# First attention of a hybrid block: units taken in pairs, in a written order, with the next batch's normalization in parts

## The chip, the cores and the metric

The kernel runs on one core of a Trainium2 chip. The metric is the device time of one execution in microseconds (us). Three executions gave 4361.11, 4361.49 and 4366.51 us, so the median is 4361.49. One more execution was taken by the hardware profiler; it is the one that all views of the profile show.

The core has several engines that run side by side, each through its own list of instructions: TensorE (PE in the profile; its weight loads are listed apart as PEld) multiplies matrices into PSUM, VectorE (DVE), ScalarE (ACT) and GpSimd (POOL) work on rows of data, and SyncE (SP) issues the transfers from and to memory. An instruction waits until what it reads has been written and until the buffer that it writes is free.

## The reference

The input x has 8 batches of 512 tokens of 256 features, all in float32. Four residual sublayers follow one another. The change is in the first:

```python
x = x + attn_a(_layernorm(x), Wq, Wkv_down, Wk_up, Wv_up, Wo)   # 8 heads of 64, one latent of 64
x = x + ffn(_layernorm(x), ...)      # two layers of local attention and a gated feedforward
x = x + attn_b(_layernorm(x), ...)   # 16 heads of 16
x = x + ffn(_layernorm(x), ...)

def attn_a(x, Wq, Wkv_down, Wk_up, Wv_up, Wo):
    q = (x @ Wq.T).reshape(b, t, 8, 64)
    kv_latent = x @ Wkv_down.T                       # b, t, 64
    k = (kv_latent @ Wk_up.T).reshape(b, t, 8, 64)
    v = (kv_latent @ Wv_up.T).reshape(b, t, 8, 64)
    attn = softmax(einsum('bqhd,bkhd->bhqk', q, k) * 64 ** -0.5)
    out = einsum('bhqk,bkhd->bqhd', attn, v).reshape(b, t, 512)
    return out @ Wo.T
```

## The kernel before

**Stages.** The eight batches go in two groups of four. For each group the stages run one behind the other: first attention, two layers of local attention and feedforward, second attention, the two layers again. Every stage is a generator of steps, and the last steps of a stage call `ahead()`, which runs single steps of the opening (`head()`) of the next one. What a stage's Python code emits first is first in an engine's list unless the scheduler, which places instructions by their dependences and the order in which they were emitted, finds something that can go earlier. `order_keeper` (line 245) overrides that: inside `with kept_order():` every instruction is tied to the one before it on its engine, in the order of the text. First attention doesn't use it in the kernel before.

**First attention** (`attention_a`, lines 311 to 485). The keys' and the queries' matrices are folded into one, and so are the values' and the output's, so a head's scores are a product of 64 folded query columns with the latent, and its values are the latent weighted by the probabilities. For each batch a `prologue` prepares three tiles: `latT` (latent, features on the partitions), `lat` (tokens on the partitions) and `qT` (folded queries). It yields after each part: the layer norm (statistics line 279, the inverse root on POOL line 267, scaling line 287), two transpositions with their copies (lines 299 and 353), the latent (358, 360), its transposition (364, 366) and four products for `qT` (374, 377). All of them share one PSUM buffer, `ps_mm`, with the projection.

**A unit** is two heads of 128 query rows against all 512 keys. A batch has 4 x 4 = 16 units, a group has 64. A unit has five parts:

- `scores`: two matmuls (line 393) into a tile `s`; the negated maximum of both heads by one DVE reduction (397); two exponentials on ACT (241, through the helper `function`), which also give the sums;
- `divide`: a DVE reciprocal of the two sums (409) and two multiplications on ACT (411);
- `turn`: eight 128x128 transposes on PE (418) into a tile `ppt`, and one DVE copy to `pt` (420);
- `values`: eight pairs of matmuls (429) into a quarter of the PSUM tile `o`; every fourth unit copies the full `o` to `oT` on ACT (439);
- `project`: every fourth unit multiplies `oT` with the folded output matrix (447) into `pp`, and adds that to x on DVE (448).

**The order** is one unit to a step. In step n the code emits `divide` of unit n-1, `scores` of unit n, `turn` of unit n-2, one piece of the next batch's prologue, `values` of unit n-3 and `project` of unit n-4:

```python
if step % each == 2 and step // each + 1 < len(batches):
    pieces = prologue(batches[step // each + 1])
for part in (1, 0, 2, 3, 4):
    at = step - part
    if 0 <= at < len(units):
        got[at] = units[at][part](*got.get(at, ()))
    if part == 2:
        next(pieces, None)
```

**Buffers.** PSUM: `s` and `ppt` share three buffers (`ps_s`), `o` has one, `mm` (prologue and projection) has one. In SBUF: `p` (probabilities) has three buffers, `pt` three, `two` (latT, oT and others) seven, `sums` three.

**Rotation tables** (`rotation_tables`, line 217) are for the local attention of the next stages. They are made once, between the opening and the steps of the first stage: two transfers, into `raw` (a buffer of the tag `p`) and `sc` (of the tag `two`), and eight DVE multiplications (227) in one run.

Of the kernel before, what the change touches and what calls it, by code (L numbers as in the profile page):

```python
# [17 lines left out]
P = 128  # L18
# [20 lines left out]
GELU_TABLES = "gelu_and_others"  # L39
Piece = namedtuple("Piece", "heavy first act second dve late", defaults=(None, None, None, None, None))  # L40
Unit = namedtuple("Unit", "n product inverse error refine masks squares masked highest exponentials turn keep_turned values project")
ISSUE_ORDER = mybir.DependencyInfo(mybir.DependencyClass.NoSync, mybir.DependencyReason.DATA)
WAIT = mybir.DependencyInfo(mybir.DependencyClass.Sync, mybir.DependencyReason.SCHED_ONLY)

# [2 lines left out]
def kernel(  # L47
# [168 lines left out]

    def rotation_tables():

        raw = pool.tile([P, 4, NT, HD], F32, tag="p", name="raw", bufs=3)
        nc.sync.dma_start(raw, rope.rearrange("c (t p) d -> p c t d", p=P))  # L220
        sc = pool.tile([P, DEPTH, 4, HD], F32, tag="two", name="sc", bufs=7)
        nc.sync.dma_start(
            sc.rearrange("p l c d -> p (l c d)"), f_scale.rearrange("l c d -> (l c d)").partition_broadcast(P)
        )
        for l in range(DEPTH):
            for c in range(4):
                nc.vector.tensor_mul(tabs[l][:, c], raw[:, c], sc[:, l, c].unsqueeze(1).to_broadcast([P, NT, HD]))

    tabs = [const.tile([P, 4, NT, HD], F32, name=f"tab{l}") for l in range(DEPTH)]

    phase = {"start": None, "last": [], "gates": False, "opening": False}
# [59 lines left out]
    def layernorm(halves, dst, name):  # L291

        normalize_rows(halves, dst, *row_statistics(halves, name)[1:])
# [17 lines left out]
    def attention_a(batches, g):  # L311
# [3 lines left out]
        def fold():  # L315
# [16 lines left out]
            for half in range(2):  # L332
# [8 lines left out]
                for odd in range(2):  # L341
                    rows = slice(odd * HD, (odd + 1) * HD)
                    nc.vector.tensor_copy(wvo_a[rows, 2 * half : 2 * half + 2, :], pw[rows, odd])

        def prologue(b):

            n = f"a{b}"
            yr = pool.tile([P, NT, D], F32, tag="yr", name=f"yr_{n}", bufs=1)
            layernorm([xs[b]], [yr], n)
            yield  # L350
            yT = pool.tile([P, 2, T], F32, tag="hT", name=f"yT_{n}")
            for k in range(2):
                nc.scalar.copy(yT[:, k, :], transposed(ps_mm, halves_of(yr), k, f"pyt_{n}_{k}"))
                yield

            pd = ps_mm.tile([P, T], F32, tag="mm", name=f"pd_{n}")
            for k in range(2):
                nc.tensor.matmul(pd, lhsT=wd_a[:, k, :], rhs=yT[:, k, :], start=(k == 0), stop=(k == 1))
            latT = pool.tile([P, T], F32, tag="two", name=f"latT_{n}", bufs=7)
            nc.vector.tensor_copy(latT, pd)  # L360
            yield
            pl = ps_mm.tile([P, NT, HD], F32, tag="mm", name=f"pl_{n}")
            for t in range(NT):
                nc.tensor.transpose(pl[:, t, :], latT[:HD, t * P : (t + 1) * P], ident[:HD, :HD])
            lat = pool.tile([P, NT, HD], F32, tag="lat", name=f"lat_{n}")
            nc.scalar.copy(lat, pl)
            yield
            qT = big([P, 4, T], f"qT_{n}")
            if b == batches[0]:
                fold()  # L370
            for m in range(4):
                pq = ps_mm.tile([P, T], F32, tag="mm", name=f"pq_{n}_{m}")
                for k in range(2):
                    nc.tensor.matmul(
                        pq, lhsT=wqk_a[:, k, m * P : (m + 1) * P], rhs=yT[:, k, :], start=(k == 0), stop=(k == 1)
                    )
                nc.scalar.copy(qT[:, m, :], pq)
                state[b] = qT, latT, lat
                yield

        def unit(b, i, u):

            n = f"a{b}_{i}_{u}"

            def scores():
                qT, latT, lat = state[b]
                if u == 0:
                    state["sums"] = pool.tile([P, H], F32, tag="sums", name=f"sums_{n}", bufs=3)
                sums = state["sums"]
                s = ps_s.tile([P, 2, T], F32, tag="s", name=f"s_{n}")  # L390
                for odd in range(2):
                    rows = slice(odd * HD, (odd + 1) * HD)
                    nc.tensor.matmul(  # L393
                        s[:, odd], lhsT=qT[rows, u, i * P : (i + 1) * P], rhs=latT[rows, :], start=True, stop=True
                    )
                nm = pool.tile([P, 2], F32, tag="nm", name=f"nm_{n}", bufs=4)
                nc.vector.tensor_reduce(nm, s, AX.X, ALU.max, negate=True)  # L397
                p = pool.tile([P, 2, T], F32, tag="p", name=f"p_{n}", bufs=3)
                for odd in range(2):
                    h = 2 * u + odd  # L400
                    function(
                        p[:, odd], s[:, odd], AF.Exp, bias=nm[:, odd : odd + 1], accum_out=sums[:, h : h + 1]
                    )
                return p, sums, lat

            def divide(p, sums, lat):

                some = sums[:, 2 * u : 2 * u + 2]
                nc.vector.reciprocal(some, some)  # L409
                for odd in range(2):  # L410
                    nc.scalar.activation(p[:, odd], p[:, odd], AF.Identity, scale=some[:, odd : odd + 1])  # L411
                return p, lat

            def turn(p, lat):
                ppt = ps_s.tile([P, 2, NT, P], F32, tag="s", name=f"ppt_{n}")
                for odd in range(2):
                    for k in range(NT):
                        nc.tensor.transpose(ppt[:, odd, k, :], p[:, odd, k * P : (k + 1) * P], ident)  # L418
                pt = pool.tile([P, 2, NT, P], F32, tag="pt", name=f"pt_{n}", bufs=3)
                nc.vector.tensor_copy(pt, ppt)  # L420
                return pt, lat

            def values(pt, lat):
                if u == 0:
                    state["o"] = ps_o.tile([P, 4, P], F32, tag="o", name=f"o_{n}")
                o = state["o"]
                for k in range(NT):
                    for odd in range(2):
                        nc.tensor.matmul(  # L429
                            o[odd * HD : (odd + 1) * HD, u, :],  # L430
                            lhsT=lat[:, k, :],
                            rhs=pt[:, odd, k, :],
                            start=(k == 0),
                            stop=(k == NT - 1),
                        )
                if u < 3:
                    return ()
                oT = pool.tile([P, 4, P], F32, tag="two", name=f"oT_{n}", bufs=7)
                nc.scalar.copy(oT, o)
                return (oT,)  # L440

            def project(oT=None):
                if oT is None:
                    return
                pp = ps_mm.tile([P, D], F32, tag="mm", name=f"pp_{n}")
                for k in range(4):
                    nc.tensor.matmul(pp, lhsT=oT[:, k, :], rhs=wvo_a[:, k, :], start=(k == 0), stop=(k == 3))
                nc.vector.tensor_add(xs[b][:, i, :], pp, xs[b][:, i, :])

            return scores, divide, turn, values, project  # L450

        units = [unit(b, i, u) for b in batches for i in range(NT) for u in range(4)]
        each = NT * 4
        def steps(ahead):
            tables_of(EXP_TABLES)
            got, pieces = {}, iter(())
            for step in range(len(units) + 4):
                if step % each == 2 and step // each + 1 < len(batches):
                    pieces = prologue(batches[step // each + 1])
                for part in (1, 0, 2, 3, 4):  # L460
                    at = step - part
                    if 0 <= at < len(units):
                        got[at] = units[at][part](*got.get(at, ()))
                    if part == 2:
                        next(pieces, None)
                if step > len(units) - 6:
                    ahead[0]()
                yield

# [1 line left out]
        rest = steps(follower)  # L471

        def head():
            yield from prologue(batches[0])
            while phase["gates"]:
                yield
            for _ in range(EARLY_STEPS):
                next(rest)
                yield

        def run(ahead):
            follower.append(ahead)
# [1234 lines left out]
```

## Time and profile before

| what | value | where it is from |
| --- | --- | --- |
| median of three runs | 4361.49 us | the times |
| the profiled execution | 4372.94 us | the times |
| its span | 4371.1 us | the profile's first line |
| PE busy in the whole span | 4122.6 us, 94% | busy time of the engines |
| first attention, first group (27 to 308 us): PE, DVE, ACT busy | 277.9, 190.6, 201.7 us of 281 | busy time by stretches |
| first attention, second group (2195 to 2480 us): PE, DVE, ACT busy | 282.7, 192.1, 202.0 us of 285 | the same |
| the exponentials, line 241, p from s and nm | 256 of 682 ns | costliest groups |
| the divisions, line 411 | 256 of 720 ns | costliest groups |
| the maxima, line 397 | 128 of 1223 ns | costliest groups |
| the copies of the transposes, line 420 (60 to 290 us) | 55 of 1214 ns | groups of a window |
| the copies of o, line 439 (60 to 290 us) | 14 of 582 ns | groups of a window |

The span is the time from the first to the last instruction of the profiled execution, and the execution's own time has 1.8 us around it. The two stages of first attention are 566 of 4371 us. A table of stretches gives, for a stretch of time, how long each engine was busy in it and how many instructions it ran; a group puts all instructions of one line and shape together; the chain lists what the end of a stretch waited for, followed back. In all of them `PE s_a L393 x4` means four matmul instructions of line 393 into the tile s_a.

### The profile page before, as it was taken

Reading aid. Unit: us, or ns where it says so; the run is one execution under the profiler, and the core shown is the slowest. Engines: PE = TensorE matmul, PEld = TensorE weight load, DVE = VectorE, ACT = ScalarE, POOL = GpSimd, SP = SyncE. Lnnn points to the kernel's source line nnn. Section 1 sums busy time; section 2 is a strip of 40 time slices with the busy share of each in tenths; the row PEclk is TensorE's granted clock in tenths of the full one; section 3 lists DMA queues with packets and bytes.
Section 4 is the critical chain, followed back from the end, with each engine's and each line's share of the span. In section 5 each row is a group of like instructions: output and inputs, shape, how many; then the busy total and the mean of one; then the engine's idle time right before and its main releaser. Section 6 shows DMA issues by size and latency. Waiting matters only on the chain.

```text
span 4371.1 us, 70487 instructions
## 1 busy us (share of the span) xinstructions
PE 4122.6 (94%) x26580; PEld 2578.8 (59%) x26580; DVE 3069.1 (70%) x7505; ACT 2686.5 (61%) x6316; POOL 1144.6 (26%) x1140
## 2 busy tenths in 40 slices
PE   8999999999998899999999999999999988999999
PEld 5666656655555466566566666566555554665665
DVE  6678737746999887377466786477379997864773
ACT  6777517616989675276167775276179896752761
POOL 0014314312222343143200242143122223422431
PEclk9999999999999999999999999999999999999999
DMA  2000000000000000000100000000000000000000
GB/s 83 1 23 4 23 3 23 3 25 21 2 1 1 20 4 7 3 23 14 53 30 1 20 4 24 23 3 24 5 21 1 1 1 20 4 6 23 3 4 24
DMA packets 51091, 63.36 MB, mean 14 GB/s; under 512 B 6336, under 2 KB 45504, under 8 KB 50752
## 3 DMA queue, kind: packets, MB, share of 16 engines
q1 hardware_dynamic: 50752, 58.85, 4.1%
q8 instruction: 211, 3.46, 0.3%
q14 instruction: 128, 1.05, 0.1%
HBM read 46.28 MB, written 4.19 MB: 12 GB/s over the span
## 4 chain that ended last, share of the span: by engine, by line
PE 67%; DVE 21%; ACT 10%; issue 1%; POOL 1%; DMA 0%; SPq 0%; POOLq 0%; ACTq 0%; DVEq 0%
PE pu_g1x L1042 3%; PE pu_g0y L1042 3%; PE pu_g1y L1042 3%; PE pu_g0x L1042 3%; PE s_a L393 3%; PE o_a L429 3%; PE ppt_a L418 3%; ACT r_b L241 2%; PE pqk_f1x L514 2%; PE pqk_f0x L514 2%; PE pqk_f1y L514 2%; PE pqk_f0y L514 2%; DVE pt_b L1389 2%; PE ppt_b L1384 2%; ACT num_b L241 2%; DVE r_b L1335 2%
## 5 line engine op out<-in xcount | busy, mean ns | idle before, releaser
L1384 PE MATMUL ppt_b<-ident,num_b 128*128 128x128 f32 x1280 | 223.5, 291 | 88.0 <-DVE pt_b L1389 65.3
L1384 PEld LDWEIGHTS ppt_b<-ident,num_b 128*128 128x128 f32 x1280 | 137.6, 143 | 273.4 <-ACT num_b L241 98.7
L241 ACT ACTIVATE num_b<-num_b,most_b 128x512 f32<-128x512 f32 (+3 forms) x512 | 280.7, 552 | 22.0 <-POOL most_b L1364 21.7
L1389 DVE COPY pt_b<-ppt_b 128x512 f32<-128x512 f32 (+1 forms) x352 | 224.3, 637 | 28.5 <-PE ppt_b L1384 27.8
L241 ACT ACTIVATE p_a<-s_a,nm_a 128x512 f32<-128x512 f32 x256 | 173.5, 682 | 105.1 <-DVE nm_a L397 101.9
L1331 DVE TENSOR_TENSOR t_b<-den_b,r_b 128x1024 f32<-128x1024 f32 (+1 forms) x176 | 197.5, 1122 | 45.4 <-ACT r_b L241 44.9
L1354 DVE CUSTOM_DVE_ANT_0 num_b<-num_b,r_b 128x512 f32<-128x512 f32 (+3 forms) x512 | 226.2, 490 | 1.9 <-POOL num_b L1347 1.9
L1347 POOL TENSOR_TENSOR num_b<-num_b,causal 128x256 f32<-128x256 f32 (+2 forms) x176 | 174.0, 988 | 186.3 <-ACT num_b L1341 185.7
L1312 PE MATMUL den_b<-st_b,st_b 18*128 18x384 f32 (+3 forms) x1024 | 208.5, 472 | 0.4 <-ACT num_b L1341 0.4
L397 DVE TENSOR_REDUCE nm_a<-s_a 128x2 f32<-128x1024 f32 x128 | 156.4, 1223 | 70.6 <-PE s_a L393 70.6
L1335 DVE SCALAR_TENSOR_TENSOR r_b<-t_b,r_b 128x1024 f32<-128x1024 f32 (+1 forms) x176 | 204.9, 1164 | 0.2
L1312 PE MATMUL dot_b<-st_b,st_b 16*128 16x384 f32 (+3 forms) x1024 | 189.6, 472 | 6.2 <-ACT yT_b L1190 4.4
L411 ACT ACTIVATE p_a<-p_a,sums_a 128x512 f32<-128x512 f32 x256 | 171.9, 720 | 26.5 <-DVE sums_a L409 26.5
L241 ACT ACTIVATE r_b<-den_b 128x1024 f32<-128x1024 f32 (+1 forms) x176 | 165.7, 941 | 35.1 <-PE den_b L1312 17.5
L241 ACT ACTIVATE p_f0y<-p_f0y,nm_f0y,rn_f0y 128x256 f32<-128x256 f32 (+1 forms) x256 | 143.7, 563 | 63.2 <-DVE nm_f0y L653 63.2
L1341 ACT ACTIVATE num_b<-dot_b 128x1024 f32<-128x1024 f32 (+1 forms) x176 | 164.6, 935 | 28.3 <-PE dot_b L1312 28.3
L241 ACT ACTIVATE p_f1y<-p_f1y,nm_f1y,rn_f1y 128x256 f32<-128x256 f32 (+1 forms) x256 | 143.7, 564 | 61.3 <-DVE nm_f1y L653 61.3
L1364 POOL TENSOR_SCALAR most_b<-most_b 128x2 f32<-128x2 f32 (+2 forms) x176 | 34.0, 193 | 557.1 <-DVE most_b L1354 541.8
L241 ACT ACTIVATE p_f0x<-p_f0x,nm_f0x,rn_f0x 128x256 f32<-128x256 f32 (+1 forms) x256 | 143.7, 563 | 57.7 <-DVE nm_f0x L653 57.7
L241 ACT ACTIVATE p_f1x<-p_f1x,nm_f1x,rn_f1x 128x256 f32<-128x256 f32 (+1 forms) x256 | 143.7, 564 | 56.3 <-DVE nm_f1x L653 56.3
L241 ACT ACTIVATE r_b<-r_b 128x1024 f32<-128x1024 f32 (+1 forms) x176 | 172.4, 980 | 5.6
L556 POOL TENSOR_TENSOR ro_f1x<-ro_f1x,rs_f1x 128x512 f32<-128x512 f32 x64 | 80.2, 1274 | 355.5 <-DVE sums_f1x L726 182.0
(356 smaller groups left out, 11230.4 us busy)
## 6 DMA issues: line engine op xcount, KB each, us to landing
x<-in_x SPq DMA_DIRECT2D x8, 512.0 KB
out<-x SPq DMA_DIRECT2D x8, 512.0 KB
wf_0x<-in_f_wqkv SPq DMA_DIRECT2D x2, 1536.0 KB
wf_0y<-in_f_wqkv SPq DMA_DIRECT2D x2, 1536.0 KB
wf_1x<-in_f_wqkv SPq DMA_DIRECT2D x2, 1536.0 KB
wf_1y<-in_f_wqkv SPq DMA_DIRECT2D x2, 1536.0 KB
wg_0x<-in_f_w SPq DMA_DIRECT2D x2, 1386.0 KB
wg_0y<-in_f_w SPq DMA_DIRECT2D x2, 1386.0 KB
```

The lines of the kernel that those rows point to most:

```text
L241: i = nc.scalar.activation(out, in_, func, **more).ins
L411: nc.scalar.activation(p[:, odd], p[:, odd], AF.Identity, scale=some[:, odd : odd + 1])
L514: nc.tensor.matmul(dst.rearrange("p h d -> p (h d)"), lhsT=hTs[b][:, k, t * P : (t + 1) * P], rhs=wqkv[:, k, c * INNER : (c + 1) * INNER], ...
L1042: nc.tensor.matmul(pu[: cols.stop - cols.start, c], lhsT=w1[:, k, cols], rhs=hT[:, k, :], start=(k == 0), stop=(k == 1),)
L1312: return nc.tensor.matmul(s[:, a, m * width : (m + 1) * width], lhsT=left[at, j, past:width], rhs=right[at, j, :width], start=True, stop=True,
L1331: nc.vector.tensor_mul(t[:, :, :cols], den[:, :, :cols], r[:, :, :cols])
L1335: nc.vector.scalar_tensor_tensor(r[:, :, :cols], t[:, :, :cols], 2.0, r[:, :, :cols], ALU.subtract, ALU.mult)
L1341: nc.scalar.activation(num[:, :, :cols], dot[:, :, :cols], AF.Square, scale=-0.5)
L1347: nc.gpsimd.tensor_add(own, own, mask)
L1354: nc.vector.tensor_tensor_reduce(out=s4[:, a, m, :], in0=s4[:, a, m, :], in1=r4[:, a, m, :], scale=-1.0, scalar=LOWEST, op0=ALU.mult, op1= ...
L1384: nc.tensor.transpose(ppt[:, k, :], p[:, a, k * P : (k + 1) * P], ident)
L1389: nc.vector.tensor_copy(pt[:, a, :nblocks, :], ppt[:, :nblocks, :])
```

## The change

First attention now goes by pairs of units, 32 to a group, with eight steps to a batch, and inside a step all engines keep the order of the text. A unit's parts are cut finer (the namedtuple `UnitA`): the maxima, the inversions, the copies of transposes, the copy of o and the addition are parts of their own. In step m the pair m is new (its units are A and B below), pair m-1 is turned (C and D), pair m-2 is weighted (E and F). The text's order is: scores A, B; values E, F; maxima A, B; a part of a normalization or one table multiplication; exponentials A, B; in odd steps the copy of o; inversion A; transposes C and their copy; a piece of the prologue; divisions A; transposes D; inversion B; the copy of D's transposes; divisions B; in odd steps the projection and its addition; another piece. So a step may run two pieces of the prologue, and a prologue now starts in the fifth step of the batch before.

The prologue's layer norm has become a generator of its own (`normalized`): statistics of two tiles of tokens at a time, then scalings of two at a time, one part to a step, between the maxima and the exponentials. The eight table multiplications go into a list (`later`) that is taken from singly in the last three steps of a batch, in steps in which no normalization part is left. `raw` and `sc` take buffers of other tags. In the last steps of a stage `ahead()` is called twice for each pair step; `head()` runs one pair step where it ran two unit steps.

```diff
-        raw = pool.tile([P, 4, NT, HD], F32, tag="p", name="raw", bufs=3)
+        raw = pool.tile([P, 4, NT, HD], F32, tag="rs", name="raw", bufs=1)
...
-        sc = pool.tile([P, DEPTH, 4, HD], F32, tag="two", name="sc", bufs=7)
+        sc = pool.tile([P, DEPTH, 4, HD], F32, tag="ro", name="sc", bufs=3)
...
-        for l in range(DEPTH):
-            for c in range(4):
-                nc.vector.tensor_mul(tabs[l][:, c], raw[:, c], sc[:, l, c].unsqueeze(1).to_broadcast([P, NT, HD]))
+        def table(l, c):
+            nc.vector.tensor_mul(tabs[l][:, c], raw[:, c], sc[:, l, c].unsqueeze(1).to_broadcast([P, NT, HD]))
+        later.extend(lambda l=l, c=c: table(l, c) for l in range(DEPTH) for c in range(4))
...
+        def normalized(b):
+            some = None
+            for tokens in (range(2), range(2, NT)):
+                some = row_statistics([xs[b]], f"a{b}", tokens, some)
+                yield
+            state["yr"] = pool.tile([P, NT, D], F32, tag="yr", name=f"yr_a{b}", bufs=1)
+            for tokens in (range(2), range(2, NT)):
+                normalize_rows([xs[b]], [state["yr"]], *some[1:], tokens)
+                yield
...
         def prologue(b):
             n = f"a{b}"
-            yr = pool.tile([P, NT, D], F32, tag="yr", name=f"yr_{n}", bufs=1)
-            layernorm([xs[b]], [yr], n)
-            yield
+            yr = state["yr"]
...
+            for m in range(len(pairs) + 2):
+                new, turning, weighted = pair(m), pair(m - 1), pair(m - 2)
+                done = weighted[1] if weighted and m % 2 else None
+                following = m // each + 1
+                with kept_order():
+                    for some in new:
+                        some.scores()
+                    for some in weighted:
+                        some.values()
+                    for some in new:
+                        some.maxima()
+                    if m % each == (m < each) and following < len(batches):
+                        rows = normalized(batches[following])
+                    if next(rows, rows) is rows and later and m % each > 4:
+                        later.popleft()()
+                    for some in new:
+                        some.exponentials()
+                    if done:
+                        done.keep_values()
+                    if new:
+                        new[0].invert()
+                    if turning:
+                        turning[0].turn()
+                        turning[0].keep_turned()
+                    if m % each == 4 and following < len(batches):
+                        pieces = prologue(batches[following])
+                    next(pieces, None)
+                    if new:
+                        new[0].divide()
+                    if turning:
+                        turning[1].turn()
+                    if new:
+                        new[1].invert()
+                    if turning:
+                        turning[1].keep_turned()
+                    if new:
+                        new[1].divide()
+                    if done:
+                        done.project()
+                        done.add()
+                    next(pieces, None)
+                if m > len(pairs) - 3:
+                    ahead[0]()
+                    ahead[0]()
+                yield
...
         def head():
+            yield from normalized(batches[0])
             yield from prologue(batches[0])
             while phase["gates"]:
                 yield
-            for _ in range(EARLY_STEPS):
-                next(rest)
-                yield
+            next(rest)
+            yield
```

## The prediction

> **What bounds the kernel now.** The change touches the first attention alone, which runs twice, at about 27 to 308 us and 2195 to 2480 us. I read the busy time by stretches there first, then the chain that ended last, then the timeline, for who hands over to whom.
>
> Busy time by stretches: length; busy us of TensorE (PE), its weight loads (PEld), VectorE (DVE), ScalarE (ACT), GpSimd (POOL), each with its count of instructions; granted clock, DMA share, GB/s. Three rows from later stages are for the clock, below.
>
> ```profile
> core 0: us, PE busy (x) PEld busy (x) DVE busy (x) ACT busy (x) POOL busy (x), PEclk, DMA share, GB/s
> 150.00:180.00 30.00, 30.00 (x252) 20.10 (x252) 22.55 (x32) 25.12 (x55) 1.20 (x2) 1.00 0.00 1
> ...
> 2488.45:2491.86 3.41, 2.00 (x17) 1.23 (x14) 3.38 (x15) 0.75 (x3) 3.33 (x3) 1.00 0.00 0
> 2491.86:2495.27 3.41, 3.41 (x5) 1.35 (x5) 2.97 (x13) 3.17 (x10) 0.09 (x2) 0.50 0.00 0
> 3027.74:3031.15 3.41, 1.58 (x12) 1.22 (x10) 2.97 (x12) 3.14 (x10) 0.00 (x0) 1.00 0.01 2
> ```
>
> PE is busy all 30 us, ACT 25 and DVE 23. A busy PE may still be waiting, so the chain decides (start, length, what):
>
> ```profile
> 157.21 1.02 PE ppt_a L418 x8
> 158.24 1.02 PE o_a L429 x16
> 159.26 1.92 PE pp_a L447 x8
> 161.18 1.06 PE s_a L393 x4
> 162.24 1.02 PE ppt_a L418 x8
> 163.27 1.02 PE o_a L429 x16
> 164.29 1.06 PE s_a L393 x4
> ```
>
> Only PE stands in it: scores 1.06, transposes 1.02, values 1.02, so 3.11 us a unit (scores start at 164.22, 167.33, 170.43 in the timeline), and every fourth unit a projection of 1.92: 4 x 3.11 + 1.92 = 14.35 for four units (the timeline's scores from 213.9 to 228.2 say the same). PE binds; whatever makes it wait is paid in full.
>
> The timeline gives the hand-overs (start, length, engine, line, what; in brackets the idle time before and who ended it):
>
> ```profile
> 164.22 1.13 PE L393 MATMUL s_a<-latT_a,qT_a 64*128 64x512 f32 x4
> ...
> 165.40 1.23 DVE L397 TENSOR_REDUCE nm_a<-s_a 128x2 f32<-128x1024 f32 x1 [0.20 <-PE s_a L393]
> ...
> 166.66 0.69 ACT L241 ACTIVATE p_a<-s_a,nm_a 128x512 f32<-128x512 f32 x1
> ...
> 168.13 0.17 DVE L409 RECIPROCAL sums_a<-sums_a 128x2 f32<-128x2 f32 x1 [0.38 <-ACT p_a L241]
> 168.34 1.33 ACT L411 ACTIVATE p_a<-p_a,sums_a 128x512 f32<-128x512 f32 x2 [0.23 <-DVE sums_a L409]
> ...
> 300.73 1.23 DVE L420 COPY pt_a<-ppt_a 128x1024 f32<-128x1024 f32 x1 [0.17 <-PE ppt_a L418]
> ...
> 305.48 0.58 ACT L439 COPY oT_a<-o_a 128x512 f32<-128x512 f32 x1 [3.87 <-PE o_a L429]
> ...
> 306.12 2.00 PE L447 MATMUL pp_a<-wa,oT_a 128*128 128x256 f32 x8
> ```
>
> Scores to maximum: 1.18. Maximum to exponentials: 1.26. Two exponentials hold ACT for 1.34. Transposes (299.65 in the timeline) to their copy: 1.08. Copy of o, 0.58, and 0.06 later the projection.
>
> **What is saved.** Inside a group the trace's single matmuls start 0.109 apart (transposes, value pairs) or 0.43 (512 columns): 2 x 0.43 + 8 x 0.109 + 8 x 0.109 = 2.61 of work in the 3.11 of a unit. The other 0.50 lies at the three changes of shape (64 rows, 128x128, 64 columns): the last matmul before one holds 0.09 longer, the first behind it 0.05 to 0.10. A pair step keeps the order scores A and B, values E and F, transposes C and D (A, B new; C, D the pair before; E, F the one before that): three changes for two units, 2 x 2.61 + 0.48 = 5.70. The projection, now between transposes and scores, adds only its 8 x 0.216 = 1.73 instead of 1.92. A double step (four units) is 5.70 + 7.43 = 13.13 of PE: 1.22 under 14.35. 16 double steps in each of two stages: **-39 us**, if PE never waits. The built program's instruction order does have this order on PE.
>
> **What is added: two waits.** I lay one step out from 0, the start of A's scores. PE: A 0 to 0.96, B to 1.91, E and F to 3.80, C to 4.73, D to 5.60. DVE: maximum A at 1.18, B 1.16 later at 2.34, done at 3.57. ACT: exponentials A 2.44 to 3.78. Exponentials B could follow, but the tag p has three buffers: C and D hold two, A took the third, so B writes where C's transposes read. The waits that the built program carries name exactly this. C's last transpose starts at 4.62, lasts 0.27 (the median of the tile's rows) and hands over in 0.05 to 0.1: B's exponentials run 5.0 to 6.35.
> In odd steps the copy of o stands behind them on ACT: 6.35 to 6.93. The projection behind it on PE starts at 7.0, where PE was ready at 5.60: **1.40 of stall**. The divisions queue behind the copy (6.95 to 9.6); they are wanted by the next transposes only, 3.8 after the next start at 8.8.
> In even steps the next scores want the PSUM buffer of C's transposes (three buffers, four tiles a step): the copy starts at 3.86 + 1.08 = 4.95, lasts 1.22, hands over at 6.2, where PE was ready at 5.70: **0.50**. A plain double step thus costs 15.03, not 13.13.
>
> In steps 4 to 7 of a batch, a next batch's prologue fills part of this. Step 4: the second transposition needs the one PSUM buffer mm, whose copy stands behind B's exponentials (6.35 to 6.93): 0.9. Steps 5 and 7: the product (four matmuls, 1.72) between C and D hides most of the projection's wait, but the piece behind the projection waits for its addition (0.25 hand-over, 0.43): 0.8 and 0.9 with what remains. Step 6: 0. Together 2.65 against 3.80.
> Per stage, from step 2: one plain double step, then 2.65, 3.80, 2.65, 3.80, 2.65 and four plain: 1.9 + 15.55 + 7.6 = 25.1; two stages: **+50**.
>
> **Moved work.** Normalization by two rows of tokens (four statistics at 0.4, or two scalings at 0.35) is 0.8 of DVE between maximum B (free at 3.5) and the copy of C (4.95): hidden by 0.65. The rotation tables (2.76 for eight at 40.88) go singly into the same gap. Their tags (rs, ro for p, two) free a p buffer at the start only; SP issues as many DMAs as before. In the third batch the next stage's statistics (0.8 to 1.2 a step) use that gap up: copy of C 0.65 late once, 0.2 once: +0.9 a stage, +2. Their cover gone everywhere, 0.8 in eight steps of three batches would be at most 0.15 each beyond the gap, nothing more.
> **Opening.** The first transposes wait for four exponentials and a division. Following the first stage from its second scores (32.8) by the same durations, step 2 starts at 42.3, and PE reaches at 48.4 what it had in the before at 47.0, short of 0.88 of the prologue's transposes: 2.3 late, though 1.5 double steps should have gained 1.6: +4. In the second stage the previous feedforward's output (ten us of PE) covers the first step; two waits of 1.0 and 1.4 remain against the 1.1 there now: +1.3. Bounds 0 and +8 for both. **Drain.** Last projection 0.5, the next stage's first products waiting for their columns 0.7: +1.2 a stage, bounds -1 and +4 (the existing wait of 1.29 at 294.87 there may grow).
>
> **Sum:** -39 + 50 + 2 + 5.3 + 2.4 = **+21** against the profiled execution (span 4371.1, 4372.9 in all): 4394. That execution is 11 above the median of the runs, so the forecast goes by the median: 4361.5 + 21 = **4382**.
>
> **Two rules weighed.** The page Perfetto Trace Analysis of the Trainium skill (Identifying the Most-Contended Engine) says to judge TensorE's headroom by the share of weight loads, not by busy matmuls. The first stretch has 20.10 of 30: by it a third of PE is free, the stalls would vanish in it and the sum would be -39. The chain without a gap speaks against it; I go by the chain.
> On the clock, the trace: 2488.45 to 2491.86 is 2.00 busy of 3.41, and the next 3.41 run at 0.50; 3027.74 to 3031.15, with 1.58 busy, 8 of its 12 matmuls transposes, is followed by no drop. The page TensorE: Matmul & The Clock Gate (Part 4: PE-mode transpose) says that transposes do not count as busy in the same way. By it C, D and the stall behind them are 3.2 us of idling in each plain odd step, and its half rate would come each time. The row with eight transposes contradicts that, and I take nothing for it.
>
> **Rivals.** *PE stays fed:* were the two waits covered, the sum would be -39 and the time 4322; any wait of less than 1.22 us a double step still leaves a gain. For it: ACT and DVE have 5 and 7 us free in 30. Against it: the waits come of the order, not of the load. 7%. *The two cancel:* hand-overs overlap more than I read, the stalls are 1.2 and not 1.9 a plain double step (and 0.6 of what they are elsewhere): 50 falls to 31, the sum is +2, 4363. 15%. *The clock falls:* each odd step without a prologue, 9 a stage, loses half of a 3.41 window, 1.7: +31 on top, 4413; the shown rows put the edge between 1.58 and 2.00 modelled us of 3.41, which overlaps, so it can't be excluded; the odd step has 3.41 - 1.40 = 2.0. 5%. *The order is undone by the scheduler:* excluded by the built order.
>
> **How the numbers follow.** Forecast 73%, 4370 to 4400: hand-overs of 0.05 each way on some 50 stalls are 3, the opening and drain bounds -7 to +8. About 0.2% (8.7 us) is what this kernel's runs can tell. The range 4358 to 4403 leaves out the fed PE, some of the cancelling and most of the clock's case. Faster 0.09 (fed, 0.07, and a little of the cancelling), same 0.13 (the rest of it), slower 0.78 (forecast and clock).
>
> **What would show it.** In the chain of the after: PE broken by ACT, projections released by the copy of o some 1.4 late in plain odd steps, scores released by the copy of the transposes 0.5 late; exponentials waiting for ppt_a; scores of two units 1.9 long in one run. Wrong, if projections follow the transposes at once, if the plain double step is under 14.35, or if the clock drops in the first attention.

## The result, and the profile after

The changed kernel took 4406.1 us (median of four executions, 4394.46 to 4406.74), the kernel before 4364.0 in the same comparison (4361.11 to 4373.17). The ratio is 1.0087, with a 95% interval from 1.0063 to 1.011; a second comparison, with four executions of the changed kernel and eleven of the kernel before, gave 4403.84 against 4372.5, ratio 1.0066 (1.0049 to 1.0082). So the change makes the kernel slower, as forecast, but by more: the forecast was 4382 with a range up to 4403. The median of 4406.1 lies above that range; put on the time that the forecast started from, the two ratios give 4399 and 4390 (4361.49 times each), which lie in it. The span of the profiled execution is 4392.7 us, against 4371.1 before.

Busy time by stretches of the changed kernel (columns as above), for two double steps without a prologue, and for two stretches of 3.41 us in the opening of the first stage (PEclk is the granted clock as a share of full speed):

```profile
core 0: us, PE busy (x) PEld busy (x) DVE busy (x) ACT busy (x) POOL busy (x), PEclk, DMA share, GB/s
239.40:269.64 30.24, 26.97 (x243) 19.45 (x242) 20.43 (x25) 22.47 (x51) 0.00 (x0) 1.00 0.02 5
38.76:42.17 3.41, 1.51 (x13) 1.16 (x12) 3.06 (x8) 3.41 (x10) 0.00 (x0) 1.00 0.00 0
42.17:45.58 3.41, 3.38 (x12) 1.35 (x10) 2.50 (x4) 2.99 (x6) 0.00 (x0) 0.50 0.00 0
```

PE was busy without a pause before; now it misses 3.3 us of 30, and all engines have time to spare. Eight units take 30.24 us, where before they took 2 x 14.35 = 28.70. The chain of waits of the changed kernel over one double step (start, length, what) shows who takes over:

```profile
239.44 1.92 PE s_a L409 x8
241.35 1.90 PE o_a L455 x32
243.25 1.04 PE ppt_a L442 x8
244.29 0.02 issue
244.31 1.24 DVE pt_a L446
245.55 0.04 issue
245.59 1.99 PE s_a L409 x8
247.58 1.90 PE o_a L455 x32
249.47 0.29 PE ppt_a L442 x2
249.77 0.82 issue
250.59 1.45 ACT p_a L247 x4
252.03 0.48 ACT oT_a L465
252.52 0.04 issue
252.56 1.99 PE pp_a L471 x8
```

(A product of the code is listed as two matmuls here, a transpose as one: the scores' x8 are the four products of two units.) Twice the chain leaves PE. In the even step it runs through the copy of C's transposes (`pt_a`, 1.24) to the next scores. In the odd step it goes through B's exponentials and the copy of o on ACT to the projection. The 0.82 of "issue" ahead of B's exponentials has no named releaser; it begins behind the first two of C's eight transposes, and the other six run in it. The timeline of the same stretch has the hand-overs:

```profile
245.59 1.99 PE L409 MATMUL s_a<-latT_a,qT_a 64*128 64x512 f32 x8 [0.44 <-DVE pt_a L446]
...
250.54 1.23 DVE L446 COPY pt_a<-ppt_a 128x1024 f32<-128x1024 f32 x1 [0.58 <-PE ppt_a L442]
250.59 0.69 ACT L247 ACTIVATE p_a<-s_a,nm_a 128x512 f32<-128x512 f32 x1 [0.82 <-ACT p_a L247]
...
251.93 0.58 ACT L465 COPY oT_a<-o_a 128x512 f32<-128x512 f32 x1
...
252.56 1.99 PE L471 MATMUL pp_a<-wa,oT_a 128*128 128x256 f32 x8 [1.19 <-ACT oT_a L465]
```

The copy of C's transposes, which is named as waiting for them, starts at 250.54, and B's exponentials at 250.59: so they too start when C's last transpose is done. PE is idle 0.44 before the scores and 1.19 before the projection. Scores of every fourth unit start 15.12 us apart where there is no prologue (239.4, 254.5, 269.6, 284.7), but for the start of the third batch (e7 below).

The whole time also moves with the mean granted clock, which differs between executions of one kernel: over all comparisons the kernel before took from 4361.7 at a mean of 0.994 to 4384.1 at 0.987. To compare paths, I use distances inside a trace: from the first scores to the first `pu_g0x` in the first group, and from the first `pu_g0y` to the first `pu_g1x` around the second (`pu` is a product of the feedforward). They hold first attention, the local attention behind it, and in the second group some work ahead of it. They hold clock drops too: stretches of 3.41 us at a clock of 0.50, three in both distances of the kernel before, two in e2 and e7, four in the changed kernel, e1, e4, e6 and e8, five in e10, six in e5, seven in e3 and twelve in e9. Each can cost up to 1.7 (an estimate: half of 3.41), so sums that lie a few us apart are not told apart by the table.

| kernel | first group | second group | sum against before | ratio to before (interval) |
| --- | --- | --- | --- | --- |
| before | 491.4 | 973.4 | | |
| changed | 506.7 | 987.0 | +28.9 | 1.0087 (1.0063 to 1.011) |
| changed, second trace (e5) | 509.2 | 986.8 | +31.3 | 1.0066 (1.0049 to 1.0082) |
| e1: four buffers | 489.6 | 969.8 | -5.4 | 0.9976 (0.9967 to 0.9986) |
| e2: copy of o between | 493.0 | 973.0 | +1.2 | 0.9985 (0.9975 to 0.9994) |
| e3: e2, split copy | 497.6 | 976.9 | +9.7 | 1.0014 (1.0005 to 1.0023) |
| e4: no kept order | 499.8 | 987.0 | +22.1 | 1.0052 (1.0032 to 1.0072) |
| e6: e1 and e2 | 485.8 | 963.2 | -15.7 | 0.9949 (0.9935 to 0.9963) |
| e7: next stage late | 503.2 | 982.7 | +21.2 | 1.0035 (1.0022 to 1.0049) |
| e8: e6 and e7 | 485.8 | 963.3 | -15.7 | 0.9958 (0.9944 to 0.9972) |
| e9: normalization whole | 517.3 | 996.8 | +49.4 | 1.0112 (1.0098 to 1.0126) |
| e10: e6, projection in o's bank | 479.1 | 959.7 | -26.0 | 0.9951 (0.9938 to 0.9965) |

### The profile page after: what moved, and what is told of

It reads as the page before. It is cut to its first block, busy times and chain, and to the rows that moved or that the text cites. A ratio compares the mean times of both kernels' runs of the same rounds, so it can differ in the third digit from the quotient of the medians.

```text
span 4392.7 us, 70588 instructions
## 1 busy us (share of the span) xinstructions
PE 4094.1 (93%) x26580; PEld 2581.5 (59%) x26580; DVE 3066.5 (70%) x7505; ACT 2680.0 (61%) x6316; POOL 1144.0 (26%) x1140
## 4 chain that ended last, share of the span: by engine, by line
PE 64%; DVE 22%; ACT 11%; issue 2%; POOL 1%; DMA 0%; SPq 0%; POOLq 0%; ACTq 0%; DVEq 0%
PE pu_g0y L1110 3%; PE pu_g1x L1110 3%; PE pu_g0x L1110 3%; PE pu_g1y L1110 3%; PE s_a L409 2%; PE o_a L455 2%; ACT r_b L247 2%; PE pqk_f1x L582 2%; PE pqk_f0x L582 2%; PE pqk_f0y L582 2%; PE pqk_f1y L582 2%; ACT num_b L247 2%; DVE pt_b L1457 2%; PE ppt_b L1452 2%; DVE r_b L1403 2%
## 5 line engine op out<-in xcount | busy, mean ns | idle before, releaser
L446 DVE COPY pt_a<-ppt_a 128x1024 f32<-128x1024 f32 x128 | 156.1, 1220 | 51.1 <-PE ppt_a L442 49.8
```

The lines of the kernel that those rows point to most:

```text
L446: nc.vector.tensor_copy(got["pt"], got.pop("ppt"))
```

## The experiments

All of them start from the changed kernel. A plain double step is two pair steps, so four units, without a piece of a prologue or work of the next stage.

**e1, a fourth buffer for the probabilities.** My theory was that the tag p with its three buffers holds B's exponentials back.

```diff
-                got["p"] = p = pool.tile([P, 2, T], F32, tag="p", name=f"p_{n}", bufs=3)
+                got["p"] = p = pool.tile([P, 2, T], F32, tag="ro" if u == 3 else "p", name=f"p_{n}", bufs=3)
```

> The changed kernel with a fourth buffer for the probabilities (every fourth unit takes a buffer of the tag ro, which is idle in first attention). The order of the text is kept. Theory (B's exponentials wait for C's transposes, the copy of o stands behind them, the projection behind that): B's exponentials follow A's at once, the copy of o ends 0.1 behind the transposes of D, and the 1.2 to 1.4 us of wait before the projection falls to 0.0 to 0.2. With the fourth buffer the scores' PSUM buffers also come free in another order, so the 0.5 before the next scores should go too: plain double step 13.2 to 13.4 instead of 15.12, about 20 of them in both stages, -36 us: 4370 +- 8. Rival (ACT and DVE are simply too full for a pair step, or the hand-overs are longer): the double step stays above 14.8 and the time above 4398.

The plain double step fell from 15.12 to 13.77 (scores at 240.57 and 254.34), the kernel to 4363.17 against 4374.1 before. In its timeline B's exponentials follow A's at once, but the projection still waits 0.35:

```profile
249.09 0.69 ACT L247 ACTIVATE p_a<-s_a,nm_a 128x512 f32<-128x512 f32 x1 [0.86 <-DVE nm_a L415]
249.77 0.68 ACT L247 ACTIVATE p_a<-s_a,nm_a 128x512 f32<-128x512 f32 x1
...
250.44 0.69 ACT L247 ACTIVATE p_a<-s_a,nm_a 128x512 f32<-128x512 f32 x1
251.10 0.69 ACT L247 ACTIVATE p_a<-s_a,nm_a 128x512 f32<-128x512 f32 x1
251.76 0.59 ACT L465 COPY oT_a<-o_a 128x512 f32<-128x512 f32 x1
...
252.41 1.99 PE L471 MATMUL pp_a<-wa,oT_a 128*128 128x256 f32 x8 [0.35 <-ACT oT_a L465]
```

The rival, that ACT and VectorE are too full for a pair step, is out: the same work runs 1.35 us faster with one more buffer. The even step took 5.71, so the wait of the scores went too, as expected. I missed the remainder: in the odd step the maxima start late, behind the copies of the step before, so the exponentials and the copy of o do as well.

**e2, the copy of o between the exponentials of A and B.** Here the buffers stay at three.

```diff
-                    for some in new:
+                    for some in new[:1]:
                         some.exponentials()
                     if done:
                         done.keep_values()
+                    for some in new[1:]:
+                        some.exponentials()
```

> The changed kernel with the copy of o between the exponentials of A and those of B; three buffers for the probabilities as before. Theory: the copy fills the time in which ACT waits for C's transposes anyway, and the projection no longer waits (1.4 to 0.0); the wait of the next scores for the copy of C's transposes (0.5 to 0.6 in even steps) stays. Plain double step 13.7, 20 of them, -27 us: 4379 +- 8. Rival (it is the load of ACT, not the place in its order): no change, 15.1 and 4406.

Measured: 13.67 a plain double step, as expected (13.7). The projection no longer waits, the scores still wait 0.45 in the timeline. B's exponentials wait as before, but nothing that PE needs soon stands behind them. The timeline of its double step:

```profile
252.21 1.99 PE L409 MATMUL s_a<-latT_a,qT_a 64*128 64x512 f32 x8 [0.45 <-DVE pt_a L446]
...
256.27 0.58 ACT L465 COPY oT_a<-o_a 128x512 f32<-128x512 f32 x1
...
257.21 0.69 ACT L247 ACTIVATE p_a<-s_a,nm_a 128x512 f32<-128x512 f32 x1 [0.35 <-ACT oT_a L465]
...
257.83 1.89 PE L471 MATMUL pp_a<-wa,oT_a 128*128 128x256 f32 x8
```

The time, 4369.78, is just under the expected 4371 to 4387. The distances in the trace went down by 27.7, the expected 27, so the path did what the theory says; the clock differs between executions.

**e3, the copy of C's transposes in two halves.** This run has e2's edit too.

```diff
+                ppt = got.pop("ppt")
+                for part in range(parts):
+                    heads = slice(2 * part // parts, 2 * (part + 1) // parts)
+                    nc.vector.tensor_copy(got["pt"][:, heads], ppt[:, heads])
...
-                        turning[0].keep_turned()
+                        turning[0].keep_turned(2)
```

> As the run before it, and the copy of C's transposes in two halves (one for each head), so that the first half starts four transposes earlier. Theory: the copy ends at 5.6 instead of 6.2 in the step, where PE wants the buffer at 5.7: the second wait goes as well, 13.1 to 13.3 a plain double step, 4367 +- 8. This would show that PE's own work is the 13.13 that was worked out from the removed changes of shape. Rival (PE's own work is nearer 14.35, no saving from the order): the double step cannot come under 14.

A miss: 13.82, slower than without the split. Its timeline:

```profile
250.31 1.97 PE L442 MATMUL ppt_a<-ident,p_a 128*128 128x128 f32 x16
...
251.44 1.29 DVE L449 COPY pt_a<-ppt_a 128x512 f32<-128x512 f32 x2 [0.86 <-PE ppt_a L442]
...
252.87 0.70 PE L409 MATMUL s_a<-latT_a,qT_a 64*128 64x512 f32 x2 [0.60 <-DVE pt_a L449]
```

The first half still starts 1.13 behind the first transpose, as the whole copy did: it waited for all eight. In the trace only the last of the eight raises a semaphore, so nothing could release the first half sooner. The two halves, one behind the other, take 1.29 instead of 1.23, and the scores wait 0.60. The first half did not start earlier, so this run says nothing on PE's own work; e6 does.

**e4, no kept order.** The `with kept_order():` around the pair steps is replaced by `if True:`.

> The changed kernel without the kept order inside the steps: the same parts in the same text order, but the scheduler places them. In the built program the copy of o and the division of A then stand ahead of B's exponentials on ACT, and the statistics of the next batch go early. Theory: the projection's wait goes (copy done at about 5.4), B's exponentials come later (6.1 to 7.45) and hold the second scores of the next step by some 0.3 beyond the 0.5: plain double step about 14.0, 4384 +- 10. Rival (the written order is what a pair step lives on): slower than the changed kernel, above 4410.

It came out between the two: 4394.59, ratio 1.0052. Plain double steps at 13.66 show that the scheduler's placing of the copy of o ahead of B's exponentials does what e2 does. But it also lets pieces slip: the last product of a prologue moved behind the first scores of the next batch, and the projection ahead of it waited 0.29 for the PSUM buffer, behind exponentials on ACT. The third batch of four double steps took 69.3 (16.63, 13.67, 17.98, 21.07) where it took 72.1 with the order kept, but the second took 71.4 against 69.1. By the distances this run lies 7 to 9 us under the changed kernel's two traces: what the scheduler saves in the plain steps it mostly loses again elsewhere.

**e5, the changed kernel again.** No edit; it separates the clock from the path.

> The changed kernel itself once more, beside more runs of the kernel before on one chip. So far its runs lie at 4394.5 (mean granted clock 0.993) and 4406 (0.989), and runs of the kernel before at 4365.4 (0.993) and 4380 (0.988 to 0.989). Theory: at one and the same granted clock the changed kernel is 26 to 32 us slower, and the rest of the +42 first measured is the difference of clock between the executions compared; ratio 1.006 to 1.008; the plain double step is 15.1 in this trace too, and no clock drop lies in a plain odd step. Rival (the stalls of the odd steps pull the clock down in some executions): a trace with drops between the double steps, and a distance of 40 or more at equal clock.

The second trace has the same double steps (15.12, 17.72, 21.16). At a mean granted clock of 0.989 the changed kernel took 4404.9 to 4406.7 and the kernel before 4375.1 to 4378.4; the distance is some 28 us, and +31.3 by the distances of the trace. So about ten of the first +42 go with the clock of the executions compared. The rival is wrong for the plain steps: no drop lies there in either trace. Both traces have one in the opening of the first group (at 42.2 and 39.4 us), and this one has another in the third batch:

```profile
186.20:189.60 3.40, 1.48 (x10) 1.16 (x12) 3.40 (x7) 3.38 (x10) 0.30 (x2) 0.99 0.00 0
189.60:193.00 3.40, 3.40 (x12) 1.07 (x10) 2.24 (x3) 2.56 (x7) 0.00 (x0) 0.50 0.02 5
```

After a stretch with PE busy 1.48 of 3.40, the next has a clock of 0.50; the double step takes 19.44 where it took 17.79 in the first trace.

**e6, both: four buffers, and the copy of o between the exponentials.** The edits of e1 and e2 together.

> The changed kernel with both: a fourth buffer for the probabilities, and the copy of o between the two pairs of exponentials. With the fourth buffer alone the scores no longer waited (5.71 for an even step) and the projection still waited 0.35; with the copy moved alone the projection didn't wait and the scores waited 0.52. Theory: both together leave PE no wait in a plain double step: 5.70 + 5.62 + 1.82 = 13.14, the work that was worked out beforehand as 13.13. Against the fourth buffer alone -0.6 in some 18 double steps, -11 us: ratio to the kernel before 0.994 to 0.996. Rival (ACT cannot keep up with 13.1): a wait appears elsewhere, 13.5 or more.

13.15 us a plain double step, 4350.54 against 4372.5. Its stretches and its chain:

```profile
224.05:250.35 26.30, 26.30 (x243) 19.39 (x242) 20.11 (x25) 21.37 (x50) 0.00 (x0) 1.00 0.03 6
```

```profile
224.10 1.92 PE s_a L409 x8
226.02 1.90 PE o_a L455 x32
227.92 1.90 PE ppt_a L442 x16
229.81 1.92 PE s_a L409 x8
231.73 1.90 PE o_a L455 x32
233.63 1.90 PE ppt_a L442 x16
235.53 1.73 PE pp_a L471 x8
```

The first row is busy time by stretches (PE first): the same 243 matmuls that took 30.24 us take 26.30, without a pause. The chain is PE alone again, and a double step is 1.92 + 1.90 + 1.90 twice and 1.73. This is what the pair order saves when nothing makes PE wait: 14.35 - 13.15 = 1.20. It lies where the prediction put it, in the groups: 1.92 for scores that took 2 x 1.06, 1.90 for transposes and for values that took 2 x 1.02 each, and 1.73 for the projection that took 1.92.

**e7, the next stage's opening held back.** The VectorE instructions that `ahead()` emits are tied behind the last one of the step that emits them.

```diff
+                        before = [i for i in made[-400:] if i.engine == mybir.EngineType.DVE][-1]
                         ahead[0]()
+                        for i in nc.cur_bb.bb.instructions[start:]:
+                            if i.engine == mybir.EngineType.DVE:
+                                tc.add_manual_dep(i, before.name, ISSUE_ORDER, reason="late")
```

> The changed kernel, with the VectorE instructions of the next stage's opening (its statistics and scalings, which the scheduler had put into the third batch of first attention) tied behind the last VectorE instruction of the step that emits them, so they run in the last four steps. Theory: in the third batch of each group the first two double steps took 15.39 and 17.79 against 15.12 elsewhere; they fall to 15.1 each, -2.9 a group, -5.9 in all; the last double steps and the next stage's opening lose 0 to 2 a group: 2 to 6 us faster than the changed kernel. Rival (the 2.9 have another cause): the two double steps stay as they are.

The third batch's first two double steps fell from 15.39 and 17.79 to 15.12 each, in both groups. That is 5.9 in all. The distances in the trace fell by 7.7 against the first trace of the changed kernel, which has two clock drops more; the kernel took 4388.99, where the changed kernel took 4403.84 in the same comparison, more than the expected 2 to 6, at a higher clock (0.990 to 0.994 against 0.989 to 0.992). What it was is in the chain of the changed kernel:

```profile
180.52 1.01 POOL rstd_a L273
181.53 0.99 POOL rstd_f0x L273
182.51 0.02 issue
182.54 0.41 DVE y_0x L293
182.95 1.13 DVE pt_a L446
```

The scheduler had put not only the next stage's statistics there but also a scaling, `y_0x`. It waits for the inverse root on POOL (2.60 idle on VectorE), and the copy of the transposes stands behind it. The run holds back statistics and scalings alike, so it shows that the next stage's VectorE work is the cause; how much of it is the scaling's wait is read from this one trace.

**e8, e6 with e7's edit.**

> All three together: fourth buffer, copy of o between the exponentials, next stage's VectorE work late. Theory: as the fourth buffer with the copy between, with the third batch's first two double steps at 13.2 as well (there 14.6 and 14.2 with the fourth buffer alone): -1 to -5 against that, ratio to the kernel before 0.993 to 0.996. Rival (the late work costs as much at the end as it frees): no difference to the run with two edits.

The double steps of the third batch came down to 13.15, from 13.26 and 15.06 in e6, but the time did not: the distances are the same (-15.7), and 4355.62 against 4350.54 for e6 in the same comparison isn't a gain. The late work costs at the end of the stage what it freed: from the last batch's fourth double step to the last projection it takes 38.5 instead of 36.3. That rival held.

**e9, the normalization in one piece.** `normalized` calls `layernorm` and yields once.

> The changed kernel with the next batch's normalization in one piece (statistics, inverse root on POOL, scalings) between maxima and exponentials of one step, where the change has it in four parts over four steps. Theory: in that step VectorE is held for four statistics (4 x 0.41), the round over POOL (some 1.5) and four scalings (4 x 0.35), about 4.5 us behind the maxima, where the gap is 0.65 to 1.4; the copy of C's transposes comes some 3.1 late and the next scores with it. Three batches a group: 2 x 3 to 4 and 1 x 1 to 2, 7 to 10 a group, +14 to +20 us over the changed kernel: ratio to the kernel before 1.009 to 1.012, and in a batch's first double step 17 to 19 instead of 15.12. Rival (the parts are not what hides it; VectorE has room anyway): no difference, 1.006 to 1.007.

As expected in size: ratio 1.0112 (11 to 20 us above the two ratios of the changed kernel), +18 to +21 us by the distances against its two traces, and double steps of 19.36, 20.61, 17.74 and 20.60 where a normalization falls. But not all of it is the wait that I had worked out: in this trace the clock drops in first attention at 40.5, 112.2, 187.2, 2238.7 and 2378.6 us, for 27.3 us in all, where the first trace of the changed kernel has one drop of 3.4. Half of 27.3 - 3.4 is 12, so up to 12 of the 18 to 21 us may be the clock; that it falls because PE idles longer isn't shown. Either way this trace is 18 to 21 us longer without the parts, inside a kept order.

**e10, e6 with the projection in o's PSUM buffer.**

```diff
-                got["pp"] = pp = ps_mm.tile([P, D], F32, tag="mm", name=f"pp_{n}")
+                got["pp"] = pp = ps_o.tile([P, 4, P], F32, tag="o", name=f"pp_{n}").rearrange("p k c -> p (k c)")[:, :D]
```

> The version with fourth buffer and copy of o between the exponentials, and the projection written into the PSUM buffer of o (empty once o is copied) instead of the one that the prologue's pieces use. Theory: in steps 5 and 7 of a batch the piece behind the projection no longer waits for its addition, 0.52 each time: the two double steps with a prologue 16.77 and 21.01 become 16.25 and 20.5, three batches in two groups: -6 us; ratio to the kernel before 0.992 to 0.995. Rival (the piece then waits for its own buffer's copy on ACT, behind the divisions): no difference to the version before it.

The double steps with a prologue fell from 16.77 and 21.01 to 15.95 and 20.16, by 0.8 each instead of 0.5, and the distances by 10.3. The median is 4346.84 against 4368.08; the ratio, 0.9951, is no better than e6's, and its executions had a clock of 0.988 to 0.992 where those of the kernel before beside it had 0.990 to 0.994. At 0.990, it took 4346.8 and the kernel before 4372.9 and 4374.1. Whether it beats e6 is therefore shown by the trace alone, not by the ratios. That e6 beats both kernels is shown by both.

## Why the prediction was right, and where it was not

**The saving of 39** was right. Without waits a double step is 13.15 (e6), predicted 13.13.

**The two waits** were right in place, cause and size. The projection waits for the copy of o, that for B's exponentials, and those for C's transposes. By starts, the projection comes 1.35 behind the end of D's group (252.56, where 249.41 + 0.93 + 0.87 = 251.21), predicted 1.40; the scores 0.52 late (steps of 6.22 and 5.70), predicted 0.50. Counted from the start of the odd step's scores (245.59), B's exponentials start at 5.00, the copy of o at 6.34 and the projection at 6.97, predicted 5.0, 6.35 and 7.0. The double step is 15.12 instead of 15.03. e1 removes the cause and e2 its consequence, and both remove most of the wait. With prologue, the second batch cost +2.03 more than before (69.14 against 67.11), predicted -4 x 1.22 + 3.80 + 2.65 = +1.57.

**The third batch** is the term that was mis-sized: "+0.9 a stage" for the next stage's statistics, measured 15.39 + 17.79 - 2 x 15.12 = 2.94, and 4.59 where the clock dropped. I counted statistics that take up VectorE's time; I did not ask what else of the next stage the scheduler would bring along. e7 showed that this work is the cause; in the trace it is mainly a scaling that waits for POOL, with the copies queued behind it.

**Opening and drain** were +5.3 and +2.4 with wide bounds. The first four double steps of the first group are 70.38 against 67.13 before, +3.25, where the terms gave -4.88 + 4.55 + 4 = +3.67; up to 1.7 of the 3.25 is a clock drop at 42.17 that has no counterpart before. So that term came near by luck: without the drop the opening would have cost about 1.5, and the prediction had no drop in it. In the second group they are 73.89 against 70.81, +3.08 where the terms gave +0.97. That 2.1 was not followed up by a run. From the last batch's fourth double step to the first `pu` of the next feedforward it is +2.8 a group, predicted -1.22 + 1.9 + 1.2 = +1.9.

**The sum** was +21; by double steps the traces give 15.4 and 15.2, so +30.5. Of the missing 10, the third batch is 4, the second opening 2, the two drains 2, and the rest lies in small differences. Another ten or so in the first comparison are the clock of the executions.

**The rivals.** "PE stays fed" was wrong for this change, but it named what was to be had: e6 feeds PE. The clock was priced at 1.7 in each odd step and did not drop there; it dropped in the opening, and in e5 in the third batch. The drop in the opening is no chance of one execution: all ten traces with the kept order have a stretch at 0.50 that starts between 39.3 and 42.2 us, and neither the kernel before nor e4 has one there. The prediction called a drop in first attention a sign of being wrong; it is a loss of up to 1.7 us each time beside the stalls, not in place of them.

**The two rules of the Trainium skill.** By the share of weight loads (Perfetto Trace Analysis, Identifying the Most-Contended Engine; the page names it beside the share of the peak arithmetic) e6 would have a quarter of PE left, 19.39 of 26.30. What the prediction drew from it, that the stalls would vanish in the free third, did not come: 15.12 against 13.13. Whether that quarter can be had, no run shows, and a chain without a gap doesn't rule it out: the kernel before had such a chain too, at 20.10 of 30, and the grouping still took 1.20 off PE's 14.35. Under the rule that transposes do not count as busy in the same way (TensorE: Matmul & The Clock Gate, Part 4: PE-mode transpose), taken as the prediction took it, every plain odd step would have been followed by half clock; no plain odd step of either trace was. The drops at 42.17 and 189.60 followed stretches with 1.51 and 1.48 busy of 3.41, against 1.58 without a drop before, but busy time alone doesn't decide: there is the drop after 2.00 that the prediction showed, and in the changed kernel the stretch from 1390.44 to 1393.85 has 1.49 busy and the next one keeps its full clock.

## What to carry to other kernels

In an order written out by hand a missing buffer makes everything behind the waiting instruction wait, as B's exponentials did here: before one writes an engine's order, one should follow each instruction's buffer to its last reader, and put what another engine wants next ahead of the instruction that must wait. Grouping work of one shape on the binding engine saved 8% of a double step here, and 1.97 us were lost against those 1.20 to two waits of order; it came back with one more buffer and one moved copy. Work that a scheduler is free to place from the next stage belongs in the cost of a kept order, with all that it waits for.

## What the runs showed of the hardware

The two halves of a copy that read different parts of one PSUM tile both ran behind the last of the eight transposes that wrote it (0.86 idle, as with one copy); only that transpose raises a semaphore in this program, so the run doesn't show whether the tile could be read sooner. The mean granted clock of one kernel's executions ranged from 0.987 to 0.994 with the time going from 4384.1 to 4361.7: a spread of 22 us without any edit, as large as the effects studied. The drops of stages that no edit touched differ from trace to trace: in the second attention of the first group, e1 had drops at 1365.5, 1375.7 and 1389.4 us, where the changed kernel had none between 1274 and 1482. The drop in the opening, between 39.3 and 42.2 us in all ten traces with the kept order and in no other, is the one that goes with the change. What decides which stretch loses its clock stayed open.
